# Routed experts after a recurrent layer: two of three groups store their results by tile and gather them by index

## The chip, the cores and the metric

The kernel runs on one core of a Trainium2 chip. The time is device time in microseconds (us) of one execution; "before" is the median of 12 runs. The profile describes one execution taken by the hardware profiler. Engines: TensorE (PE, matmuls; PEld, its weight loads), VectorE (DVE), ScalarE (ACT), GpSimd (POOL), SyncE (SP, here only a queue that issues transfers). Transfers run on 16 DMA engines, whichever queue issues them.

## The reference, cut to what matters

The input is x, 8 sequences of 1024 tokens with 256 features. A first layer (norms, a recurrence along the sequence, a channel mix) is added to x. Then every token is routed to 4 of 32 experts:

```python
x = x + attn_layer(layernorm(x), ...)
xt = layernorm(x).reshape(-1, 256)
gates = sigmoid(xt @ expert_sel.T)                  # 8192 tokens x 32 experts
sel_val, sel_idx = top_k(gates, 4)
gate_full = zeros.at[rows, sel_idx].set(sel_val)
scores = relu(einsum('nd,edf->nef', xt, keys))      # 256 -> 128 per expert
scores = scores * gate_full[:, :, None]
out = einsum('nef,efv->nv', scores, values)         # 128 -> 256, summed over experts
x = x + out
```

Only the chosen four experts of a token need be computed, since the gate of the others is zero. All data is float32.

## The kernel before, in words

The 8192 tokens are 16 blocks of 512. A block passes through the first layer (`norm_a` to `channel_end`), which writes the running x of the block to DRAM (`acc`), and through the routing (`norm_d`, `gates_of`, `rows_of`), which gives each token four rows, one per chosen expert. `post` (line 558) then scatters the normalized token to these rows of a DRAM array `xs`: one indirect transfer on POOL per 128 tokens and choice, 16 per block. In `xs` every expert has a region of its own, so an expert's tokens lie one behind the other. With each token go its place (token number times 4) and its row numbers.

The blocks form three groups of 10, 5 and 1 (`GROUPS`, line 31; the numbers behind the size set the pace). When all blocks of a group are routed, `tile_table` (line 592) works out from the counts which expert and which row of `xs` every tile of 256 rows starts at. A group has 96, 56 and 24 tiles. The last 16 tiles of a group are made of two halves of 128 rows, each with its own expert, so that less is padding; the rows of a tile that are not tokens of its expert are computed as well.

`experts` (line 709) runs the tiles. `fetch` loads a tile from `xs` (SP); `turn` transposes it (TensorE, line 794) and ScalarE (in the first group VectorE) copies it to `xgT` (line 878); `keys` copies the expert's key weights (VectorE, line 785); `hidden` and `result` are the two matmuls (lines 806 and 822), two steps apart, with ScalarE's `hs` (line 884) and `yg` (line 888) between and behind them. `places` (line 762) works out on VectorE, from the row numbers that came with each row, which of the token's four choices it is, and so its row in `ys`, an array with 4 rows per token in token order. `send` (line 832) scatters the 256 results to `ys` with two indirect transfers on POOL, of 128 rows of 1 KB each; rows that are no tokens carry a place out of bounds and are not written.

`combine` (line 892) adds up: for each part of 128 tokens it loads the 4 x 256 results of each token from `ys`, which lie side by side, in one plain transfer of 512 KB (line 909, SP), and adds them with their gates to the block's `acc` (four VectorE instructions, line 917); a finished block goes to the output (line 930; the last block in four pieces, line 927). The sums of a group come after all its tiles, since any tile may hold any token's result.

The order of the work is written as generators: `advance` is called between the pieces of the block loop and moves the background streams (tiles and sums of the groups) by their pace; behind the last block, `drain` runs on until all are done. The tiles of a group follow those of the group before, its sums the sums of the group before. The tile layer then schedules the instructions, each engine runs its own in order, and semaphores join them. `pinned` keeps the tiles of one group in order on each engine; `apart` declares that scatters of one kind need not wait for one another. A read of `ys` waits for all writes of that group's `ys`.

Of the kernel before, what the change touches and what calls it, by code (L numbers as in the profile page):

```python
# [8 lines left out]
F32 = mybir.dt.float32  # L9
BF16 = mybir.dt.bfloat16  # L10
U32 = mybir.dt.uint32
I32 = mybir.dt.int32
AF = mybir.ActivationFunctionType
ALU = mybir.AluOpType
# [5 lines left out]
P = 128  # L20
EPS = 1e-5
WKV_EPS = 1e-8
TOP = 4
# [5 lines left out]


GROUPS = ((10, 6, 2.2, 4, 0.5), (5, 4, 1.6, 4, 0.7), (1, 2, 1.0, 2, 1.0))


@with_exitstack
def rwkv_then_routed_experts(
# [101 lines left out]
    for g, members in enumerate(groups):  # L137
        gt = len(members) * TB
        r = const.tile([P, NE], F32, name=f"region1_{g}")
        nc.gpsimd.iota(  # L140
            r,
            pattern=[[gt + TS, NE]],
            base=TS + 1,
            channel_multiplier=0,
            allow_small_or_imprecise_dtypes=True,
        )
        region1.append(r)
        n_tiles.append(gt * TOP // TS + NE // 2)
        regions.append(NE * (gt + TS))
        xs.append(dram.tile([regions[g] + TS, DX], F32, name=f"xs_{g}"))  # L150
        ys.append(dram.tile([gt * TOP, D], F32, name=f"ys_{g}"))
    tile_no = const.tile([P, 1], F32, name="tile_no")
    nc.gpsimd.iota(
        tile_no, pattern=[[0, 1]], base=0, channel_multiplier=1, allow_small_or_imprecise_dtypes=True
# [340 lines left out]
    def rows_of(i):  # L495
        m = mine[i]
        g = group_of[i]
        chosen = m["chosen"]

        ps = ps_a.tile([P, NT, NE], F32, tag="a", name=f"rank_{i}")  # L500
        prior = counted.get(g)
        nc.tensor.matmul(ps, before, chosen, start=True, stop=False, skip_group_check=True)
        for s in range(1, NT):
            nc.tensor.matmul(
                ps[:, s:, :],
                ones,
                chosen[:, : NT - s, :],
                start=False,
                stop=(s == NT - 1 and prior is None),
                skip_group_check=True,  # L510
            )
        total = p2.tile([P, NT, NE], BF16, tag="total", name=f"total_{i}")
        if prior is not None:
            nc.tensor.matmul(ps, ones, prior, start=False, stop=True, skip_group_check=True)

        key = p2.tile([P, NT, NE], F32, tag="key", name=f"key_{i}")
        nc.vector.tensor_tensor(key, ps, region1[g][:, None, :].to_broadcast([P, NT, NE]), ALU.add)
        nc.vector.tensor_tensor(key, key, chosen, ALU.mult)
        k8 = p2.tile([P, NT, 8], F32, tag="k8", name=f"k8_{i}")
        for t in range(NT):  # L520
            nc.vector.max(k8[:, t, :], key[:, t, :])

        tc.keep_in_program_order(
            nc.vector.tensor_scalar(
                m["x3"][:, :, D], place, float(groups[g].index(i) * TB * TOP), None, ALU.add
            )
        )
        nc.vector.tensor_copy(m["x3"][:, :, D + 1 :], k8[:, :, : TAGS - 1])
        row = p2.tile([P, NT, TOP], U32, tag="row", name=f"row_{i}")
        nc.vector.tensor_scalar(row, k8[:, :, :TOP], -1.0, None, ALU.add)  # L530
        chosen_sum = p2.tile([P, NE], F32, tag="csum", name=f"csum_{i}")
        nc.vector.tensor_reduce(chosen_sum, chosen.rearrange("p t e -> p e t"), AX.X, ALU.add)
        if prior is not None:
            nc.vector.tensor_tensor(chosen_sum, chosen_sum, prior[:, 0, :], ALU.add)
        nc.vector.tensor_copy(total, chosen_sum[:, None, :].to_broadcast([P, NT, NE]))
        counted[g] = total
        m["row"], m["key"], m["k8"] = row, key, k8
# [54 lines left out]
    def tile_table(g):  # L592
# [71 lines left out]
        for k in range(3):  # L664
# [7 lines left out]
        live = small([3], "live")  # L672
        nc.vector.tensor_scalar(live, past[:, :, NE - 1], -1.0, 1.0, ALU.mult, ALU.add)

        say = small([2, 2], "say")
        nc.vector.tensor_copy(say[:, 0, :], what[:, 0, 1:])
        half = small([2], "half")
        nc.vector.tensor_scalar(half, what[:, 1, 1:], float(-regions[g]), None, ALU.add)
# [3 lines left out]
        whole = small([2, 2], "whole")  # L682
        nc.vector.tensor_copy(whole, what[:, :, 0:1].to_broadcast([P, 2, 2]))
        nc.vector.tensor_scalar(whole[:, 1, 1:], whole[:, 1, 1:], float(H), None, ALU.add)
        nc.vector.tensor_tensor(whole, whole, say, ALU.subtract)
        nc.vector.scalar_tensor_tensor(
            say, whole, live[:, 0:1], say, ALU.mult, ALU.add
        )
        yield


        stride = len(groups[g]) * TB + TS
        diag = small([2, P], "diag", BF16)
        ps = ps_a.tile([P, 2, P], F32, tag="a", name=f"all_{g}")
        for k in range(2):
            nc.vector.tensor_scalar(diag[:, k, :], ident, say[:, 0, k : k + 1], None, ALU.mult)
        nc.tensor.matmul(ps, ones, diag, start=True, stop=True)
        limit = p1.tile([P, 2, P], F32, tag="limit", name=f"limit_{g}")
        nc.vector.tensor_scalar(limit, ps, float(stride), float(stride + TS // 2), ALU.mult, ALU.add)

        ps = ps_a.tile([4, P], F32, tag="a", name=f"tr_say_{g}")
        nc.tensor.transpose(ps, say.rearrange("p a b -> p (a b)"), ident)
        table = keep.tile([4, P], I32, name=f"table_{g}")
        nc.vector.tensor_copy(table, ps)
        tables[g] = table, limit

# [2 lines left out]
    def experts(g, pause):  # L709
# [1 line left out]
        table, limit = tables[g]  # L711
        T = n_tiles[g]

        EXPERT, ROW = range(0, 4, 2)
        most = {EXPERT: NE - 1, ROW: regions[g]}
        whole_only = T - NE // 2
        ahead = {}

        def value(t, column, half, engine):

            start = t - t % RUN if t < whole_only else t - (t - whole_only) % RUN
            if (engine, start, column, half) not in ahead:
                stop = min(start + RUN, whole_only if t < whole_only else T)
                _, ahead[engine, start, column, half] = nc.values_load_multi_w_load_instructions(
                    table[column + half : column + half + 1, start:stop],
                    engines=[engine],
                    min_val=0,
                    max_val=most[column],
                    skip_runtime_bounds_check_because=WHY,
                )  # L730
            return ahead[engine, start, column, half][t - start]

        def parts(t):

            return [(0, 0, SJ)] if t < whole_only else [(j, j, j + 1) for j in range(SJ)]

        latest = {}

# [13 lines left out]
        def fetch(t):  # L752
            tag = "xT" if blocks_over and t % 2 else "xg"
            xg = p3.tile([P, SJ, DX], F32, tag=tag, name=f"xg_{g}_{t}")
            for half, j0, j1 in parts(t):
                at = value(t, ROW, half, ET.SP)
                n = j1 - j0
                source = xs[g][bass.ds(at, n * P), :].rearrange("(p j) d -> p j d", j=n)
                nc.sync.dma_start(out=xg[:, j0:j1, :], in_=source)  # L759
            return xg  # L760

        def places(t, xg):
# [53 lines left out]
        def result(t, hs):  # L816
# [12 lines left out]
                    )  # L829
            return ps, last  # L830

        def send(yg, to):
            for j in range(SJ):
                s = nc.gpsimd.indirect_dma_start(  # L834
                    out=ys[g],
                    out_offset=bass.IndirectOffsetOnAxis(ap=to[:, j : j + 1], axis=0),
                    in_=yg[:, j, :],
                    in_offset=None,
                    bounds_check=len(groups[g]) * TB * TOP - 1,
                    oob_is_err=False,  # L840
                )
                apart("store", g, s)
# [15 lines left out]
        for step in range(T + 2 * STAGE):  # L858
# [15 lines left out]
            if step < T:  # L874
                xgT = turned[step] = p3.tile([P, KC, TS], F32, tag="xgT", name=f"xgT_{g}_{step}")

                move = nc.scalar.copy if g else nc.vector.tensor_copy
                after(move(xgT, trx), signal)  # L878
                to[step] = places(step, xg)
            if step < T:  # L880
                ks[step] = keys(step)
            if 0 <= h < T:
# [2 lines left out]
            if 0 <= r < T:  # L885
                tag = "k2" if blocks_over and r % 2 else "yg"
                yg = p3.tile([P, SJ, D], F32, tag=tag, name=f"yg_{g}_{r}")
                after(nc.scalar.copy(yg, po), signal)  # L888
                send(yg, to.pop(r))
            yield  # L890

    def combine(g):
# [10 lines left out]
        def gather(j):  # L903
            i, t = parts[j]
            tags = ("g", "xn", "xa") if blocks_over else ("g",)
            g4 = p2.tile([P, TOP, D], F32, tag=tags[j % len(tags)], name=f"g_{i}_{t}")
            first = TOP * (groups[g].index(i) * TB + t * P)
            rows = ys[g][first : first + TOP * P, :].rearrange("(p k) d -> p k d", k=TOP)
            nc.sync.dma_start(out=g4, in_=rows)  # L909
            got.append((j, [g4[:, k, :] for k in range(TOP)]))  # L910

        def add():
# [167 lines left out]
    for i in range(total_blocks + 1):  # L1080
# [2 lines left out]
                post(len(waiting))  # L1083
                beside(expert_group(g, *pace))
        period(i)
        if i < 2:
            clear(i + 1)
        elif i < 6:
            load_experts(i - 2)
    blocks_over.append(True)  # L1090
    post(len(waiting))
# [47 lines left out]
```

## Time and profile before

| | |
|---|---|
| median of 12 runs | 1382.01 us (1380.36 to 1387.47) |
| the profiled execution | 1384.78 us |
| its span | 1383.1 us |
| busy in the span: PE, DVE, ACT, POOL | 92%, 70%, 42%, 49% |
| indirect transfers on POOL | 352 sends to `ys`, 256 scatters to `xs` |
| plain gathers of sums on SP | 64 |
| PE busy of the 283 us from 1100 | 201.5 us |

Engine rows of the page give tenths of busy time in 40 slices of the span. A group's row gives the line, the engine, the operation and how often; then busy time in us and the mean of one in ns; then the idle time in front and what ended most of it. A row by stretch gives the bounds, the length, the busy time and number of instructions of PE, PEld, DVE, ACT and POOL, the granted TensorE clock (1 is full), the share of the DMA engines' time in use, and GB/s. A row of the timeline gives the start, the duration, the engine and line, and in brackets the idle time before and what ended it. The POOL time of an indirect transfer is the making of its descriptors; its data moves afterwards.

### The profile page before, as it was taken

The numbers are of one execution on the slowest core, as the hardware profiler recorded it, in microseconds if no ns is written. First come the engines' busy times: TensorE is split into PE (matmuls) and PEld (weight loads), VectorE is DVE, ScalarE is ACT, GpSimd is POOL, SyncE is SP. The second block draws the span as 40 slices with busy tenths as digits, with TensorE's granted clock in tenths as the row PEclk, the third lists the DMA queues.
The fourth block names the chain that finished last, engine by engine and source line by source line (L and its number), as shares of the span: only waits on it lengthen the run. The fifth ranks groups of instructions, "written<-read, shape, count | busy, mean of one in ns | idle before, by whom it ended". The sixth has DMA issues, their size and how long they took to land. (4 is left out here: it accounts for less than half of the span.)

```text
span 1383.1 us, 19513 instructions
## 1 busy us (share of the span) xinstructions
PE 1267.1 (92%) x5590; PEld 916.2 (66%) x5590; DVE 971.4 (70%) x3166; ACT 586.6 (42%) x1122; POOL 671.5 (49%) x678
## 2 busy tenths in 40 slices
PE   6999999999999999998999999999998578688772
PEld 2566666666666666665877787787875367577662
DVE  6957878878878878878666667766656847356484
ACT  3354444444444544543444434434434144345431
POOL 2011433333423422535476667667656437777763
PEclk9999999999999999999999999999998879899896
DMA  9990221421411211213465455445337669798595
GB/s 326 343 287 4 86 109 46 146 103 48 150 47 43 90 47 43 90 44 121 121 196 160 146 155 189 153 144 176 109 129 254 229 216 322 275 309 275 202 310 208
DMA packets 134074, 223.06 MB, mean 161 GB/s; under 512 B 19231, under 2 KB 92229, under 8 KB 133456
## 3 DMA queue, kind: packets, MB, share of 16 engines
q1 hardware_dynamic: 102736, 151.96, 35.1%
q0 software_dynamic: 29184, 68.25, 13.4%
q10 hardware_dynamic: 2048, 1.61, 0.4%
q8 instruction: 46, 0.75, 0.2%
q14 instruction: 60, 0.49, 0.1%
HBM read 110.01 MB, written 124.28 MB: 169 GB/s over the span
## 5 line engine op out<-in xcount | busy, mean ns | idle before, releaser
L834 POOL DMA_INDIRECT ys<-yg,to x352 | 352.4, 1001 | 197.8 <-ACT yg L888 85.7
L563 POOL DMA_INDIRECT xs<-x,row x256 | 257.4, 1005 | 102.2 <-issue 85.4
L423 PEld LDWEIGHTS cm<-wval,k 128*128 128x128 f32 x1024 | 194.3, 190 | 77.0 <-issue 50.0
L244 PE MATMUL pj_f<-xT,wkey 128*128 128x512 f32 x512 | 243.9, 599 | 0.0
L423 PE MATMUL cm<-wval,k 128*128 128x256 f32 x1024 | 240.5, 379 | 2.3 <-ACT k L416 2.3
L806 PE MATMUL ph<-xgT,key 128*128 128x256 f32 (+1 forms) x896 | 190.9, 345 | 18.0 <-DVE key L785 10.2
L822 PE MATMUL po<-wexp,hs 128*128 x704 | 186.0, 387 | 5.7 <-ACT hs L884 4.9
L917 DVE SCALAR_TENSOR_TENSOR ac<-g,gate,ac 128x256 f32<-128x256 f32 x256 | 123.1, 487 | 84.7 <-DMA g<-ys 67.0
L806 PEld LDWEIGHTS ph<-xgT,key 128*128 128x128 f32 x896 | 151.5, 197 | 39.5 <-issue 16.4
L371 POOL TENSOR_TENSOR x<-x,xa 128x1024 f32<-128x1024 f32 x16 | 37.9, 2368 | 255.6 <-issue 222.8
L415 ACT ACTIVATE k<-pj_f 128x512 f32<-128x512 f32 x128 | 76.5, 598 | 195.7 <-PE pj_f L244 195.7
L822 PEld LDWEIGHTS po<-wexp,hs 128*128 128x128 f32 x704 | 125.2, 194 | 27.2 <-issue 8.1
L244 PEld LDWEIGHTS pj_f<-xT,wkey 128*128 128x128 f32 x512 | 92.9, 191 | 68.4 <-issue 65.5
L794 PE MATMUL trx<-ident,xg 128*128 128x128 f32 x704 | 110.3, 282 | 28.8 <-ACT xgT L878 18.5
L884 ACT ACTIVATE hs<-ph 128x256 f32<-128x256 f32 x176 | 68.4, 389 | 154.0 <-PE trx L794 148.6
L888 ACT COPY yg<-po 128x512 f32<-128x512 f32 x176 | 102.7, 584 | 68.9 <-DMA ys<-yg,to 67.8
L878 DVE COPY xgT<-trx 128x512 f32<-128x512 f32 x96 | 65.6, 683 | 84.5 <-PE trx L794 84.5
L794 PEld LDWEIGHTS trx<-ident,xg 128*128 128x128 f32 x704 | 89.5, 146 | 47.2 <-ACT xgT L878 21.8
L325 DVE RECIPROCAL rw<-rw 128x512 f32<-128x512 f32 x32 | 107.3, 3353 | 1.0
L785 DVE COPY key<-wexp 128x256 f32 x224 | 69.2, 319 | 45.7 <-PE ph L806 32.0
L878 ACT COPY xgT<-trx 128x512 f32<-128x512 f32 x80 | 47.0, 589 | 83.6 <-PE trx L794 83.6
L416 ACT ACTIVATE k<-k 128x512 f32<-128x512 f32 x128 | 80.6, 630 | 4.1
(162 smaller groups left out, 1735.0 us busy)
## 6 DMA issues: line engine op xcount, KB each, us to landing
xg<-xs SPq DMA_DIRECT2D x128, 264.0 KB
g<-ys SPq DMA_DIRECT2D x64, 512.0 KB
xs<-zeros SPq DMA_DIRECT2D x6, 4224.0 KB
xg<-xs SPq DMA_DIRECT2D x96, 132.0 KB
x<-in_x SPq DMA_DIRECT2D x16, 512.0 KB
acc<-x SPq DMA_DIRECT2D x16, 512.0 KB
wexp<-in_w_exp SPq DMA_DIRECT2D x4, 2048.0 KB
ac<-acc SPq DMA_DIRECT2D x16, 512.0 KB
```

What stands on the lines that cost most here:

```text
L244: nc.tensor.matmul(ps, w(c), rhs[:, c, :], start=(c == 0), stop=(c == KC - 1))
L325: inverse = nc.vector.reciprocal(rc, rc)
L416: nc.scalar.activation(k2, k2, AF.Square)
L423: nc.tensor.matmul(m["cm"][t // 2][:, t % 2, :], k2[:, t * P : (t + 1) * P], wval[:, f, :], start=(f == 0 and t % 2 == 0), stop=(f == FC - 1),
L563: s = nc.gpsimd.indirect_dma_start(out=xs[g], out_offset=bass.IndirectOffsetOnAxis(ap=m["row"][:, t, k : k + 1], axis=0), in_=m["x3"][:, t ...
L794: nc.tensor.transpose(ps[:, c, j * P : (j + 1) * P], xg[:, j, c * P : (c + 1) * P], ident)
L806: nc.tensor.matmul(ps[:, cols], key[:, c * P : (c + 1) * P], xgT[:, c, cols], start=(c == 0), stop=(c == KC - 1),)
L822: nc.tensor.matmul(ps[:, j, :], hs[:, j * P : (j + 1) * P], wexp[:, bass.ds(e, 1), KC * P :], start=True, stop=True,)
L834: s = nc.gpsimd.indirect_dma_start(out=ys[g], out_offset=bass.IndirectOffsetOnAxis(ap=to[:, j : j + 1], axis=0), in_=yg[:, j, :], in_offse ...
L878: after(move(xgT, trx), signal)
L888: after(nc.scalar.copy(yg, po), signal)
L917: nc.vector.scalar_tensor_tensor(ac, gk, routed[i][:, t, k : k + 1], ac, ALU.mult, ALU.add)
```

## The change

For groups two and three (`PLAIN = (1, 2)`):

- `ys` has the layout of `xs`: a tile's 256 results are stored in the rows that its inputs came from, with plain transfers on ScalarE's queue, one of 256 KB for a whole tile and two of 128 KB for a tile of two halves. Padding rows are stored too. Tiles that hold nothing get rows of their own behind the regions (`dead`, `PLACE`); a third pair of columns in the table gives the row.
- `places` and the `limit` table are not made, and `send` is not called.
- The row numbers of each block (`row`) are kept, and `combine` gathers a part of 128 tokens with four indirect transfers on POOL, one per choice, of 128 rows of 1 KB each, where it had one plain load on SP.

Group one is as before.

```diff
+PLAIN = (1, 2)
...
-        ys.append(dram.tile([gt * TOP, D], F32, name=f"ys_{g}"))
+        results = regions[g] + n_tiles[g] * TS if g in PLAIN else gt * TOP
+        ys.append(dram.tile([results, D], I32 if g in PLAIN else F32, name=f"ys_{g}"))
...
-        row = p2.tile([P, NT, TOP], U32, tag="row", name=f"row_{i}")
+        if g in PLAIN:
+            row = keep.tile([P, NT, TOP], U32, name=f"row_{i}")
+        else:
+            row = p2.tile([P, NT, TOP], U32, tag="row", name=f"row_{i}")
...
+        if g in PLAIN:
+
+            dead = small([2], "dead")
+            nc.vector.tensor_scalar(
+                dead, past[:, 1:, NE - 1], past[:, 0, NE - 1 : NE], None, ALU.mult
+            )
+            nc.vector.tensor_tensor(dead, dead, down, ALU.mult)
+            nc.vector.tensor_tensor(say[:, 2, :], say[:, 1, :], dead, ALU.add)
         yield
...
+        def store(t, yg):
+            for half, j0, j1 in parts(t):
+                at = value(t, PLACE, half, ET.Activation)
+                s = nc.scalar.dma_start(out=rows(ys[g], at, j1 - j0), in_=yg[:, j0:j1, :].bitcast(I32))
+                apart("store", g, s)
...
-                to[step] = places(step, xg)
+                if g not in PLAIN:
+                    to[step] = places(step, xg)
...
-                send(yg, to.pop(r))
+                if g in PLAIN:
+                    store(r, yg)
+                else:
+                    send(yg, to.pop(r))
...
-            first = TOP * (groups[g].index(i) * TB + t * P)
-            rows = ys[g][first : first + TOP * P, :].rearrange("(p k) d -> p k d", k=TOP)
-            nc.sync.dma_start(out=g4, in_=rows)
+            if g in PLAIN:
+                for k in range(TOP):
+                    nc.gpsimd.indirect_dma_start(
+                        out=g4[:, k, :].bitcast(I32),
+                        out_offset=None,
+                        in_=ys[g],
+                        in_offset=bass.IndirectOffsetOnAxis(ap=mine[i]["row"][:, t, k : k + 1], axis=0),
+                    )
+            else:
+                first = TOP * (groups[g].index(i) * TB + t * P)
+                rows = ys[g][first : first + TOP * P, :].rearrange("(p k) d -> p k d", k=TOP)
+                nc.sync.dma_start(out=g4, in_=rows)
```

More of the change, by code (lines that the diff above doesn't have):

```diff
@@ L673, in tile_table @@
         nc.vector.tensor_scalar(live, past[:, :, NE - 1], -1.0, 1.0, ALU.mult, ALU.add)
-        say = small([2, 2], "say")
+        say = small([3, 2], "say")
         nc.vector.tensor_copy(say[:, 0, :], what[:, 0, 1:])
@@ L684, in tile_table @@
         nc.vector.tensor_scalar(whole[:, 1, 1:], whole[:, 1, 1:], float(H), None, ALU.add)
-        nc.vector.tensor_tensor(whole, whole, say, ALU.subtract)
+        nc.vector.tensor_tensor(whole, whole, say[:, :2, :], ALU.subtract)
         nc.vector.scalar_tensor_tensor(
-            say, whole, live[:, 0:1], say, ALU.mult, ALU.add
+            say[:, :2, :], whole, live[:, 0:1], say[:, :2, :], ALU.mult, ALU.add
         )
-        yield
-        stride = len(groups[g]) * TB + TS
-        diag = small([2, P], "diag", BF16)
@@ L694, in tile_table @@
[L694 to L702, printed above, removed]
@@ L703, in tile_table @@
-        table = keep.tile([4, P], I32, name=f"table_{g}")
+        if g in PLAIN:
[5 more added lines that the diff above has]
+            nc.vector.tensor_tensor(say[:, 2, :], say[:, 1, :], dead, ALU.add)
+        yield
+        limit = None
+        if g not in PLAIN:
+            stride = len(groups[g]) * TB + TS
+            diag = small([2, P], "diag", BF16)
+            ps = ps_a.tile([P, 2, P], F32, tag="a", name=f"all_{g}")
+            for k in range(2):
+                nc.vector.tensor_scalar(diag[:, k, :], ident, say[:, 0, k : k + 1], None, ALU.mult)
+            nc.tensor.matmul(ps, ones, diag, start=True, stop=True)
+            limit = p1.tile([P, 2, P], F32, tag="limit", name=f"limit_{g}")
+            nc.vector.tensor_scalar(
+                limit, ps, float(stride), float(stride + TS // 2), ALU.mult, ALU.add
+            )
@@ L704, in tile_table @@
+        columns = 6 if g in PLAIN else 4
+        ps = ps_a.tile([columns, P], F32, tag="a", name=f"tr_say_{g}")
+        nc.tensor.transpose(ps, say.rearrange("p a b -> p (a b)")[:, :columns], ident)
+        table = keep.tile([columns, P], I32, name=f"table_{g}")
         nc.vector.tensor_copy(table, ps)
@@ L712, in experts @@
         T = n_tiles[g]
-        EXPERT, ROW = range(0, 4, 2)
-        most = {EXPERT: NE - 1, ROW: regions[g]}
+        EXPERT, ROW, PLACE = range(0, 6, 2)
+        most = {EXPERT: NE - 1, ROW: regions[g], PLACE: regions[g] + (T - 1) * TS}
         whole_only = T - NE // 2
@@ L727, in value @@
                     min_val=0,
-                    max_val=most[column],
+                    max_val=most[column] + (half * TS // 2 if column == PLACE else 0),
                     skip_runtime_bounds_check_because=WHY,
@@ L735, in parts, with rows @@
             return [(0, 0, SJ)] if t < whole_only else [(j, j, j + 1) for j in range(SJ)]
+        def rows(array, at, n):
+            return array[bass.ds(at, n * P), :].rearrange("(p j) d -> p j d", j=n)
         latest = {}
@@ L757, in fetch @@
                 n = j1 - j0
-                source = xs[g][bass.ds(at, n * P), :].rearrange("(p j) d -> p j d", j=n)
-                nc.sync.dma_start(out=xg[:, j0:j1, :], in_=source)
+                nc.sync.dma_start(out=xg[:, j0:j1, :], in_=rows(xs[g], at, n))
             return xg
@@ L878, in experts @@
                 after(move(xgT, trx), signal)
-                to[step] = places(step, xg)
+                if g not in PLAIN:
+                    to[step] = places(step, xg)
             if step < T:
@@ L906, in gather @@
             g4 = p2.tile([P, TOP, D], F32, tag=tags[j % len(tags)], name=f"g_{i}_{t}")
-            first = TOP * (groups[g].index(i) * TB + t * P)
-            rows = ys[g][first : first + TOP * P, :].rearrange("(p k) d -> p k d", k=TOP)
-            nc.sync.dma_start(out=g4, in_=rows)
+            if g in PLAIN:
[5 more added lines that the diff above has]
+                        in_offset=bass.IndirectOffsetOnAxis(ap=mine[i]["row"][:, t, k : k + 1], axis=0),
+                    )
+            else:
+                first = TOP * (groups[g].index(i) * TB + t * P)
+                rows = ys[g][first : first + TOP * P, :].rearrange("(p k) d -> p k d", k=TOP)
+                nc.sync.dma_start(out=g4, in_=rows)
             got.append((j, [g4[:, k, :] for k in range(TOP)]))
@@ L1085, in rwkv_then_routed_experts @@
         period(i)
-        if i < 2:
+        if i + 1 < len(groups):
             clear(i + 1)
-        elif i < 6:
+        elif 2 <= i < 6:
             load_experts(i - 2)
```

## The prediction

> **What bounds the kernel now.** I read the page first (engine shares, forty slices), then the chain that ended last, then busy time by stretch of the last 270 us, then the waits and the timelines there. Up to 1050 us TensorE is busy nearly all the time and nothing that the change touches lies there. The last quarter is different:
>
> ```profile
> span 1383.1 us, 19513 instructions
> ...
> PE   6999999999999999998999999999998578688772
> ...
> POOL 2011433333423422535476667667656437777763
> PEclk9999999999999999999999999999998879899896
> DMA  9990221421411211213465455445337669798595
> ...
> DMA ys<-yg,to 4%; DMA g<-ys 3%; PE ph L806 2%; DVE ac L917 1%; PE po L822 1%; POOL ys L834 1%; PE trx L794 1%; DMA out<-ac 1%; SPq L759 0%; DMA ac<-acc 0%; DVE key L785 0%; DMA xg<-xs 0%; ACT xgT L878 0%; SPq L909 0%; POOL xs L563 0%
> ...
> L834 POOL DMA_INDIRECT ys<-yg,to x352 | 352.4, 1001 | 197.8 <-ACT yg L888 85.7
> ```
>
> The reader is to see TensorE fall from 9 to 5 to 8 tenths in the last nine slices, and the indirect sends `ys<-yg,to` at the head of the chain. By stretch (start and end; PE, PEld, DVE, ACT, POOL busy; clock, DMA share, GB/s):
>
> ```profile
> 1125.80:1189.40 63.60, 55.29 (x300) 47.16 (x297) 42.49 (x213) 29.90 (x66) 48.46 (x48) 0.97 0.93 315
> 1189.40:1295.10 105.70, 84.70 (x491) 73.31 (x492) 48.27 (x194) 50.24 (x110) 80.98 (x82) 0.94 0.75 250
> 1295.10:1366.50 71.40, 48.69 (x278) 41.80 (x276) 49.58 (x165) 25.40 (x57) 47.72 (x47) 0.88 0.86 296
> 1366.50:1383.10 16.60, 0.00 (x0) 0.00 (x0) 7.23 (x16) 0.00 (x0) 0.00 (x0) 0.50 0.45 163
> ```
>
> POOL runs 130 indirect DMAs from 1125.8 to 1295.1: 129.4 us busy plus 130 gaps of 0.30 us is the whole stretch. Its timeline shows the pitch, 1.28 us, and the waits of this stretch show who pays:
>
> ```profile
> 1190.69 0.98 POOL L834 DMA_INDIRECT ys<-yg,to  x1 [0.30 <-issue]
> 1191.98 0.97 POOL L834 DMA_INDIRECT ys<-yg,to  x1 [0.30 <-issue]
> ```
> ```profile
> ACT yg L888 <- DMA ys<-yg,to: 67.8, 37, 11.2
> ```
>
> So the second group's 56 tiles are bound by POOL's sends: ScalarE waits 67.8 us for result buffers. The hand-over follows: last result copy of that group, first gather of its sums, last additions of all.
>
> ```profile
> 1280.50 0.59 ACT L888 COPY yg<-po 128x512 f32<-128x512 f32 x1 [2.91 <-DMA ys<-yg,to]
> ```
> ```profile
> 1295.10 0.33 SPq L909 DMA_DIRECT2D g<-ys  x1
> ```
> ```profile
> 1376.20 4.03 DVE L917 SCALAR_TENSOR_TENSOR ac<-g,gate,ac 128x256 f32<-128x256 f32 x9 [1.50 <-DMA g<-ys]
> ```
>
> Call T1 the time at which all results of the second group have landed: 1295 now. From T1 to the end now takes 88 us, because its sums are fetched by 20 plain loads of 512 KB that SP issues at 0.43 us each.
>
> **The change, part by part.**
>
> *Removed from POOL:* 112 sends of group two and 48 of group three. *Added to POOL:* 80 gathers for group two (5 blocks x 4 parts x 4) and 16 for group three. The count falls by 64, but in time it is a move: the removed ones ran beside the tiles, while no gather can start before T1, since it reads rows that any tile may have stored. In the built order of the changed kernel all 96 gathers stand at the end of POOL's queue, behind the last scatters.
>
> *T1.* Without the sends three things can hold the 56 tiles. TensorE: the result copies on ScalarE stand 2.17 us apart where nothing waits (1124.93, 1127.09), so 1124.9 + 55 x 2.17 = 1244; with the last block's gate products (1.7 us), the copy (0.6), two issues (0.9) and a landing (2.4 to 5.4 us as the sends show), T1 = 1250 to 1253. DMA: 1120 to 1280 moves 46.9 MB at 293 GB/s. The plain stores write all 256 rows of a tile, 56 x 0.262 = 14.7 MB, where the sends wrote the 10,240 real rows, 10.5 MB: 4.2 MB more. Some 3.9 MB (fetches of group three, sums of group two) may slide behind, leaving 47.2 MB: at the 345 GB/s of the fullest 10 us stretches 137 us, at the present mean 161, so the last copy comes at 1257 to 1281 and T1 at 1261 to 1286. ScalarE: a tile takes 1.35 us now; one store adds 0.43 (its issues in the first 6 us), a half tile two, so 1.8 to 2.3 us with a wait for its own copy, about TensorE's pace; 14 table loads at 0.54 to 0.6 are 8 us, mostly in slack. I take T1 = 1272, in the middle of the DMA bound, 23 us earlier than now; ends 1250 and 1286.
>
> The Trainium skill, page "DMA: Bandwidth & Descriptors", section "Issuing engines are not separate DMA queues", says that issuing from another engine saves only the issue time, usually small beside the transfer. By that rule moving the stores to ScalarE's queue would leave T1 near 1295; here the issue is what POOL is full of, and no run shows yet which of the two holds.
>
> *Gathers of group two.* The trace has no gather by index. The nearest row is the scatter by index: also 128 rows of 1 KB per instruction, pitch 1.28 us. A plain issue (0.33 to 0.43 us) is the lower bound, the longest scatter (1.91 + 0.30) the upper: over the 94 pitches below, minus 80 or plus 87 us. I take 1.28, as the scatters of both kinds agree (medians 0.962 and 0.974). First gather at 1272.1, the 80th at + 79 x 1.28 = 1373.2. Six buffers hold the gathered parts; an addition of a part takes 4 x 0.49 against 5.1 us for its gathers, so POOL is never held by them. Now the same rows come in 60 us beside the sends; that cover is gone.
>
> Page "SBUF — State Buffer", section "SBUF: two separate sides", says that a VectorE copy in a two-port mode keeps POOL from writing descriptors. Its figures, about 620 ns alone and 3100 overlapped, would add an estimated 40 x 2.5 = 100 us if each of the 40 key copies met a gather; the sends beside the same copies show a mean of 1.00 and a longest of 1.91 us.
>
> *What is queued behind a waiting addition.* On VectorE the additions of group two stand between the key copies of group three: key 5 behind two additions, keys 20 to 23 behind all 80. TensorE's later stages wait for those keys, so the third group's tiles now run at the gathers' pace, and the last four only start when the 80th gather has landed (2.4 us) and been added (0.5). Then: two key copies 0.6; TensorE 4 hidden x 0.86, 2 transposes x 0.66, 6 results x 0.86 = 9.9 at full clock (groups of four in the chain); ScalarE 1.0; two issues 0.9; landing 2.4; plus 1.7 because the clock stands at 0.50 to 0.54 after idle (1110 to 1120, 1190 to 1200). That is 16.5; with TensorE at half clock throughout 25, and 1.3 for the whole gap if POOL could go straight on. So gather 81 comes 19.4 us after gather 80: 1392.6. Third group: 15 x 1.28 = 19.2, to 1411.8.
>
> *End.* Landing 2.4, last addition 0.5, output 2.9 (now from the last addition at 1380.2 to 1383.1): 1417.6.
>
> *At nothing:* 240 small VectorE instructions that worked out places (0.16 us each) and the two limit tables are gone, a few for the third pair of table columns are new; VectorE is busy half of these stretches. The kept row tiles cost memory only. SP loses 24 loads of 0.43, behind no one.
>
> Sum: span 1417.6 against 1383.1, plus 34.5. The profiled run took 1384.78, 1.68 outside the span and 2.77 above the median 1382.01. On the median: 1416.5.
>
> **Rivals.**
>
> *Cheap gathers (not slower).* If POOL writes a gather's descriptors faster than a scatter's, the whole tail shrinks by 94 us per us of pitch. It decides at 1.28 - 34.5/94 = 0.91 us with my T1, at 1.15 with T1 = 1250. At 0.8: 1371. For it: the fall of 64 instructions and POOL being the bound. Against: both scatters cost the same whatever their target, so the work seems to be the 128 descriptors.
>
> *The sends were hidden anyway.* The DMA share is already 0.93 in the first stretch; if the larger stores fill what the sends left, T1 stays at 1290: 1416.5 + 18 = 1434. Against: 0.75 in the second stretch.
>
> *Dear gathers.* Reads of scattered rows beside busy VectorE and DMA at a pitch of 1.6: 94 x 0.32 = + 30, 1446.
>
> *Third group not held.* If its tiles finish before gather 80, the gap is 1.3: 1398. Against: the order on VectorE.
>
> **How the numbers follow.** Main case 0.68, its own range 1394 to 1431 (T1 alone gives minus 22 to plus 14). Sends hidden 0.11, dear gathers 0.09, third group not held 0.05, cheap gathers 0.07. About 0.2% (2.8 us) is what a measurement of this kernel tells from no change. Cheap gathers fall mostly below it: faster 0.06, same 0.02, slower 0.92. Range 1393 to 1446: it leaves out cheap gathers and half of the dear ones.
>
> **What would show it.** Right: POOL empty or nearly so from the last scatter to about 1272, then 80 gathers in a row near 1.28 us, a hole of some 20 us, 16 more; ScalarE's wait for `ys` gone; TensorE thin after T1 with its clock below 0.8; VectorE waiting for gathers. Wrong: a pitch below 1.15 us, a T1 above 1290 or below 1250, or no hole before the last 16.

## The result, and the profile after

The changed kernel takes 1423.11 us (median of 8 runs, 1422.06 to 1427.63) against 1383.35 us of the kernel before, measured beside it: a ratio of 1.0291, 95% interval 1.0279 to 1.0303. It is 2.9% slower. The profiled execution took 1428.24 us, its span 1426.2 us. In the changed code `turn` is at line 815, `keys` at 806, `hidden` at 827, the store at 856, `send` at 861, `xgT`, `hs` and `yg` at 905, 912 and 916, the gather by index at 940 and the addition at 957.

The page of the changed kernel, rows as in the one of before:

```profile
span 1426.2 us, 19276 instructions
...
PE   6999999999999999999999999999986788884661
...
POOL 2011343244144144172666666676663040007754
PEclk9999999999999999999999999999998799997676
DMA  9980230331321121124555455444377799977853
...
q10 hardware_dynamic: 18176, 22.59, 4.4%
...
L940 POOL DMA_INDIRECT g<-ys,row x96 | 93.2, 970 | 155.8 <-DMA ys<-yg 107.6
```

POOL, which ran at 7 tenths where the second group's tiles were sent, is now at 0 there and at 7 behind it: the work has moved from beside the tiles to behind them. The 96 gathers take 970 ns each. The last stretches, with the columns of the prediction's table (length; PE, PEld, DVE, ACT, POOL busy; clock, DMA share, GB/s):

```profile
1125.80:1189.40 63.60, 56.30 (x311) 47.33 (x309) 30.77 (x125) 31.67 (x70) 16.52 (x16) 1.00 0.98 347
1189.40:1279.60 90.20, 74.71 (x421) 63.83 (x422) 34.32 (x98) 42.68 (x94) 0.00 (x0) 0.95 0.92 306
1279.60:1401.30 121.70, 72.22 (x333) 60.31 (x331) 46.72 (x115) 30.67 (x68) 78.03 (x81) 0.75 0.67 208
1401.30:1426.20 24.90, 0.00 (x0) 0.00 (x0) 7.75 (x16) 0.00 (x0) 15.12 (x16) 0.50 0.37 106
```

In the first two, POOL runs nothing but the last 16 scatters, and the DMA engines are in use for 0.92 to 0.98 of the time; behind 1279.6 they have slack and POOL is what is full. POOL's timeline shows the three parts of the tail; these are the first two gathers, the 80th and 81st, and the last:

```profile
1279.62 0.99 POOL L940 DMA_INDIRECT g<-ys,row  x1 [107.58 <-DMA ys<-yg]
1280.91 0.96 POOL L940 DMA_INDIRECT g<-ys,row  x1 [0.30 <-issue]
...
1380.76 0.94 POOL L940 DMA_INDIRECT g<-ys,row  x1 [0.30 <-issue]
1401.29 0.94 POOL L940 DMA_INDIRECT g<-ys,row  x1 [19.58 <-issue]
...
1420.04 0.95 POOL L940 DMA_INDIRECT g<-ys,row  x1 [0.30 <-issue]
```

So: 79 pitches in 101.14 us, a hole of 20.53 us between two starts, 15 pitches in 18.75, and 6.2 us from the last start to the end of the span. The span grew by 43.1 us. T1, the start of the sums, came 15.5 us earlier (1295.1 to 1279.6); from T1 to the end it is 146.6 us instead of 88.0, which is 58.6 more.

VectorE's timeline shows what the hole is made of:

```profile
1383.83 0.48 DVE L957 SCALAR_TENSOR_TENSOR ac<-g,gate,ac 128x256 f32<-128x256 f32 x1 [0.44 <-DMA g<-ys,row]
1384.23 0.89 DVE L806 COPY key<-wexp 128x256 f32 x4
```

The key copies of tile 20 come right behind the last addition of group two; the last result copy follows at 1397.59 and its two stores at 1398.20. The second of them has landed at 1400.45, and the gathers of the third group start at 1401.29.

The waits from 1110 us to the end (us in total, times, longest):

```profile
POOL g L940 <- DMA ys<-yg: 107.6, 1, 107.6
DVE ac L957 <- DMA g<-ys,row: 79.6, 72, 13.5
...
POOL g L940 <- issue: 44.9, 84, 19.6
PE ph L827 <- DVE key L806: 42.8, 17, 6.5
...
ACT xgT L905 <- DMA xg<-xs: 20.9, 5, 9.6
...
ACT yg L916 <- DMA ys<-yg: 4.8, 2, 2.6
```

ScalarE's wait for result buffers fell from 67.8 to 4.8 us. VectorE's additions wait for the gathers, TensorE's `hidden` for the key copies behind those additions.

### The profile page after: what moved, and what is told of

Its sections match the earlier page's. It is cut to its first block, busy times and chain, and to the rows that moved or that the text cites. A ratio compares the mean times of both kernels' runs of the same rounds, so it can differ in the third digit from the quotient of the medians.

```text
span 1426.2 us, 19276 instructions
## 1 busy us (share of the span) xinstructions
PE 1281.6 (90%) x5588; PEld 925.8 (65%) x5588; DVE 945.0 (66%) x2926; ACT 586.1 (41%) x1122; POOL 603.7 (42%) x614
## 5 line engine op out<-in xcount | busy, mean ns | idle before, releaser
L861 POOL DMA_INDIRECT ys<-yg,to x192 | 190.9, 994 | 121.7 <-ACT yg L916 54.5
L827 PE MATMUL ph<-xgT,key 128*128 128x256 f32 (+1 forms) x896 | 196.9, 353 | 45.8 <-DVE key L806 43.2
L843 PE MATMUL po<-wexp,hs 128*128 x704 | 191.6, 396 | 17.0 <-ACT hs L912 13.1
L827 PEld LDWEIGHTS ph<-xgT,key 128*128 128x128 f32 x896 | 156.0, 203 | 70.7 <-issue 37.5
L940 POOL DMA_INDIRECT g<-ys,row x96 | 93.2, 970 | 155.8 <-DMA ys<-yg 107.6
L843 PEld LDWEIGHTS po<-wexp,hs 128*128 128x128 f32 x704 | 128.1, 198 | 40.5 <-ACT hs L912 17.0
## 6 DMA issues: line engine op xcount, KB each, us to landing
xs<-zeros SPq DMA_DIRECT2D x6, 4224.0 KB, 19.7
```

Source lines behind the costliest of these rows:

```text
L827: nc.tensor.matmul(ps[:, cols], key[:, c * P : (c + 1) * P], xgT[:, c, cols], start=(c == 0), stop=(c == KC - 1),)
L843: nc.tensor.matmul(ps[:, j, :], hs[:, j * P : (j + 1) * P], wexp[:, bass.ds(e, 1), KC * P :], start=True, stop=True,)
L861: s = nc.gpsimd.indirect_dma_start(out=ys[g], out_offset=bass.IndirectOffsetOnAxis(ap=to[:, j : j + 1], axis=0), in_=yg[:, j, :], in_offse ...
L940: nc.gpsimd.indirect_dma_start(out=g4[:, k, :].bitcast(I32), out_offset=None, in_=ys[g], in_offset=bass.IndirectOffsetOnAxis(ap=mine[i]["r ...
```

## The experiments

Times are compared on the chip where they were taken. Four runs (`keys_first`, `half_gathers`, `third_only`, `second_only`) fell on a chip that is slower with every kernel: the one before takes 1502.88 us there, and the block stages, which no edit touches, are longer too. Of these only ratios to the kernel before and lengths of stretches are used. The other chips give 1382.17 and 1383.65 us for the kernel before.

**The unaltered changed kernel, as a control.**

> The changed kernel once more, unaltered, beside three that differ from it in one thing each, on one chip. Its ratio to the kernel before was 1.029. Every theory expects 1.025 to 1.035, and the same three parts after the last store of group two has landed: 80 gathers 1.28 us apart (101 us), a hole of about 20 us, 16 gathers (19 us).

Measured: 1425.77 us, ratio 1.0306 (1.0286 to 1.0326). Its first gather is at 1280.32, the hole between two starts ends at 1401.84, and the last gather starts at 1420.65: the same parts as above, within 1 us. T1 itself varies more: the next experiment, whose edit acts only behind T1, has it at 1276.18.

**The key copies of group three ahead of the additions of group two.** Only the order on VectorE is altered; nothing is left out.

```diff
+                key_made[g, t] = pinned(nc.vector.tensor_copy(key, ...))
...
+                if g == 1:      # addition of part j
+                    tc.add_manual_dep(added.ins, key_made[2, min(23, 6 + 2 * j)].ins.name, NoSync, ...)
```

> The changed kernel, with the additions of group two ordered on VectorE so that all key copies of group three come before the additions of the tenth part. Theory (the 96 gathers run in series on POOL, and the last four tiles of group three wait for the 80th gather through VectorE's order): T1 stays near 1280, the 80 gathers still take 101 us, the hole before the last 16 shrinks from 20.5 us to 1 to 4, and the span falls by 16 to 19 us, from 1426 to 1407 to 1410. Rival (group three's tiles are late for another reason: DMA, the granted clock, or their fetches): the hole stays above 12 us and the time moves by less than 8 us.

> The changed kernel, with the additions of group two's part j behind the key copy of tile 6 + 2j of group three, beside the unaltered one. Theory (the hole comes from the keys behind the additions): the hole of 20 us is gone, some of it paid back in waits of the gathers for their buffers, 0 to 15 us; so 5 to 20 us less than the unaltered kernel, a ratio of 0.986 to 0.997 between the two. Rival (TensorE and the transfers of group three need that time wherever its keys stand): within 0.3% of the unaltered kernel.

Measured beside the control: 1406.09 us against 1425.77, 0.986 of it; to the kernel before 1.0177 (1.0150 to 1.0204). That is 19.7 us less, at the favourable end of what was expected. In the timeline of POOL (the gather is at line 941 here) the first and the last of 96 gathers are

```profile
1276.18 1.02 POOL L941 DMA_INDIRECT g<-ys,row  x1 [105.07 <-DMA xg<-xs]
...
1396.69 0.95 POOL L941 DMA_INDIRECT g<-ys,row  x1 [0.30 <-issue]
```

that is 120.5 us for 95 pitches, 1.27 us each: there is no hole, and no gather waits for a buffer. Between the 80th and the 81st start there is one pitch instead of the control's 19.91 us, 18.6 us less, which is nearly all of the gain. By stretch:

```profile
1276.10:1300.00 23.90, 23.90 (x149) 21.81 (x148) 10.23 (x29) 13.46 (x30) 18.31 (x19) 0.98 0.93 296
1300.00:1330.00 30.00, 26.45 (x176) 24.11 (x176) 15.86 (x44) 14.79 (x35) 22.84 (x23) 0.94 0.96 309
1330.00:1360.00 30.00, 2.33 (x11) 1.42 (x10) 10.48 (x24) 2.42 (x6) 22.84 (x24) 0.58 0.64 197
```

TensorE's last instruction of group three ends at 1333; in the changed kernel the last four of these tiles only start behind the addition at 1383.83. So the third group's tiles fit beside the gathers of the second; the hole came from the queue on VectorE, and the rival, that the time is needed anyway, falls.

On the slower chip the same edit gave 1.0074 (1.0048 to 1.0100) of the kernel before there. The hole is gone too, but POOL pays some of it back; there its waits say

```profile
POOL g L941 <- DVE key L807: 23.8, 5, 7.2
```

where the gathers stood for buffers that additions behind late key copies held. With the chip at its usual pace this wait does not appear.

**What sets the start of the gathers: the stores on another queue, and fewer bytes.**

```diff
-                at = value(t, PLACE, half, ET.Activation)
-                s = nc.scalar.dma_start(...)
+                at = value(t, PLACE, half, ET.Pool if g == 1 else ET.Activation)
+                s = (nc.gpsimd if g == 1 else nc.scalar).dma_start(...)
```

> The changed kernel, with the plain stores of group two issued on POOL's queue, which is nearly empty there, instead of ScalarE's. Theory (the start of the gathers is set by the bytes that the transfers move, 0.92 to 1.04 of their time): first gather and time within 4 us of the unaltered kernel (0.3%). Rival (it is set by ScalarE, which stands at a store until its result copy and an earlier transfer are done, while the other copies of the tiles queue behind): first gather about 15 us earlier, and so the time (ratio 0.99 to the unaltered kernel).

```diff
-                nc.sync.dma_start(out=g4, in_=rows)
-            got.append((j, [g4[:, k, :] for k in range(TOP)]))
+                nc.sync.dma_start(out=g4[:, :2, :], in_=rows[:, :2, :])
+            got.append((j, [g4[:, k, :] for k in range(TOP if g else 2)]))
```

> The changed kernel, which leaves out two of the four choices in the sums of group one: its plain loads fetch half as much, some 5.5 MB less between the last scatter and the first gather. Theory (bytes set the start of the gathers): 5.5 MB at 345 GB/s is 16 us, so the first gather 10 to 16 us earlier against the unaltered kernel, and the time too (ratio 0.989 to 0.993). Rival (ScalarE or TensorE sets it): first gather and time within 4 us.

Measured: the stores on POOL's queue 1418.14 us, 0.9946 of the control, 1.0256 (1.0239 to 1.0273) of the kernel before; with fewer bytes 1413.93 us, 0.9917 of the control. The first gathers, of the control, of the stores on POOL's queue and of fewer bytes, stand at

```profile
1280.32 0.98 POOL L940 DMA_INDIRECT g<-ys,row  x1 [106.82 <-DMA xg<-xs]
```
```profile
1267.30 1.02 POOL L940 DMA_INDIRECT g<-ys,row  x1 [4.90 <-DMA xg<-xs]
```
```profile
1265.74 0.98 POOL L940 DMA_INDIRECT g<-ys,row  x1 [99.32 <-DMA xg<-xs]
```

that is 13.0 and 14.6 us earlier than in the control. Each is from one execution; the medians fell by 7.6 and 11.8 us. I had set these two against one another, and had expected the first to move nothing. Both move T1, so neither alone was the bound. (With fewer bytes half of group one's additions are left out too, and VectorE works 46.7 us instead of 65.2 from 1125.8 to 1265. That can hardly be the cause: in the control TensorE waits for key copies for only 1.2 us before T1.) The stretch from 1125.8 to 1265, first of the control and then of the stores on POOL's queue, shows how:

```profile
1125.80:1265.00 139.20, 120.24 (x677) 102.07 (x675) 65.17 (x220) 67.90 (x151) 16.35 (x16) 0.98 0.98 341
```
```profile
1125.80:1265.00 139.20, 127.40 (x746) 110.86 (x745) 66.01 (x224) 74.88 (x166) 55.33 (x87) 0.98 0.99 356
```

The DMA share is 0.98 in one and 0.99 in the other, yet the second moved 356 GB/s instead of 341, and TensorE did 7.2 us more work in the same time. What holds the first is ScalarE at its stores. Its timeline in the changed kernel:

```profile
1239.30 0.59 ACT L916 COPY yg<-po 128x512 f32<-128x512 f32 x1
1239.92 3.79 ACTq L856 DMA_DIRECT2D ys<-yg  x2
1243.76 0.59 ACT L905 COPY xgT<-trx 128x512 f32<-128x512 f32 x1 [3.86 <-DMA xg<-xs]
```

One issue takes 0.34 to 0.41 us, but these two stores, of two halves of one result that was complete at 1239.89, last 3.79 us, and the next tile's copy comes only behind them. The trace records for which counts an instruction waits. In the changed kernel 66 of the 72 stores of group two wait, beside their own copy, for the completion count of an earlier transfer: the queues of SP and ScalarE share eight such counts. Twenty of the 72 are issued within 0.15 us of the landing of that transfer, in 17 cases one of SP's queue, and ScalarE stands idle for 31.7 us ahead of these twenty (29.6 in the control, also ahead of twenty). The second store of the rows above is one of them: a fetch of `xg` landed 0.02 us before its issue.

Added up from the timeline of the changed kernel (from the end of the ScalarE instruction ahead of a store to the end of its issue, 1125.8 to 1278 us), the 72 stores take 59.3 us of ScalarE, of which 72 x 0.38 = 27 is issue and 32 waiting; in the control 56.3 and 29. With the stores on POOL's queue these waits are off the engine that has the tiles' copies to make; POOL's transfers have counts of their own, and no store there is issued within 0.15 us of such a landing. With fewer bytes the waits are shorter (24 by the same sum).

On POOL's queue the same bytes go in fewer packets (4736 instead of 10368 for the 72 stores), but not at a lower price: from 1125.8 to 1265 the stores took 24.6% of the DMA engines' time for 12.81 MB in the control and 28.1% for 14.63 MB on POOL's queue (without its scatters), 1.92% per MB in both. What the stores' place on ScalarE costs is 9 to 13 us of T1: with the same bytes, three executions with it have T1 at 1276.2 to 1280.3, two without it at 1267.2 and 1267.3. That the waits are for the shared counts the trace shows; no run takes away the counts alone.

**Both edits.** The two diffs above in one kernel, the stores of group two on POOL's queue and the keys of group three first:

> The changed kernel with both edits: the stores of group two on POOL's queue, and the additions of group two behind the key copies of group three. If the two losses are separate, they add: first gather at about 1267 us, then 96 gathers without a hole, 95 x 1.27 = 121 us, and 6 us to the end: a span of about 1394 us, a ratio of 1.010 to the kernel before (1.005 to 1.014). Rival (the earlier gathers meet the transfers of group three, and wait for them): no better than the keys alone, 1.018.

Measured: 1398.70 us, ratio 1.0107 (1.0093 to 1.0122); gathers from 1267.16 to 1387.97 without a hole. The separate gains, 19.7 and 7.6 us, add to 27.3; from the control's 1425.77 that is 1398.5, so the two losses are separate. What is left of the loss is the 96 gathers in a row at 1.27 us behind T1.

**Half the gathers of group two, and one group alone.** These are of the slower chip.

```diff
-                for k in range(TOP):
+                for k in range(TOP if g == 2 else 2):
...
-            got.append((j, [g4[:, k, :] for k in range(TOP)]))
+            got.append((j, [g4[:, k, :] for k in range(2 if g == 1 else TOP)]))
```

> The changed kernel without the gathers and additions of the third and fourth choice of group two: 40 of 96 gathers are left out, and the output lacks those terms. Theory: what follows T1 is POOL's series, so the span falls by 40 x 1.27 = 51 us to about 1375, T1 unchanged near 1280, the 40 gathers end at about 1331, and the hole before the last 16 stays near 20 us or grows by a few, since group three's tiles now come at TensorE's pace. Rival (something else sets the time after T1): the span falls by less than 25 us.

Measured, in one run: 1487.94 us, 0.990 of the kernel before there. Group two's gathers end sooner, but then the hole is twice as long; by stretch, gathers of group two, hole, end:

```profile
1356.00:1417.40 61.40, 27.15 (x127) 22.38 (x126) 18.63 (x46) 11.67 (x26) 38.62 (x40) 0.69 0.62 191
1417.40:1459.10 41.70, 32.52 (x209) 29.08 (x207) 8.85 (x29) 19.00 (x42) 0.05 (x1) 0.95 0.62 202
1459.10:1486.00 26.90, 0.00 (x0) 0.00 (x0) 7.75 (x16) 0.00 (x0) 15.12 (x16) 0.50 0.35 98
```

The ratio is near what the theory gives (a span of 1375 against 1383.1), but not by its parts: from the first gather to the end 130.2 us passed, where the theory has 95. In the hole TensorE is busy for 32.5 of 41.7 us: more of the third group's tiles are left when the additions are done. Part of that is this chip: ScalarE stood for 24.6 us in a wait that the trace marks as remote, until 1404.6, and TensorE for 21.7 us behind it. So the size of the hole is not to be taken over, and since the changed kernel was not run here, the run does not say what a gather left out is worth.

```diff
-PLAIN = (1, 2)
+PLAIN = (2,)
```

> Only group three is stored by tile; group two keeps its sends and plain loads. Theory (group two's late gathers are the loss; the change to group three costs about what it saves): T1 is back at 1290 to 1296, group two's sums are loaded beside group three's tiles, group three's last store lands near 1360 because DMA is full there, then 16 gathers of 1.25 us and 6 us for the end: span 1380 to 1390, within 0.5% of the kernel before. Rival (storing by tile is itself what costs, whatever the group): 1395 or more.

> Only group two is stored by tile; group three keeps its 48 sends and 4 plain loads. Theory (POOL's queue after T1 sets the end): T1 near 1280, then 80 gathers and 48 sends share POOL, 128 x 1.27 = 163 us to about 1443, then 12 to 16 us for the last loads and additions: span 1450 to 1465, the slowest of all. Rival (the late gathers of group three and the hole before them are the loss): the hole goes and the span falls to 1400 to 1415.

Measured: the third group alone 1.0049 (1.0027 to 1.0072) of the kernel before, just within the theory's 0.5%; the second alone, in one run, 1550.40 us or 1.032. That lies between the theory (a span of 1450 or more, 1.048) and the rival (1415 or less, 1.023). With the second alone (`PLAIN = (1,)`) the 48 sends of group three stay on POOL among the 80 gathers, as the timeline there shows:

```profile
1400.67 0.97 POOL L940 DMA_INDIRECT g<-ys,row  x1 [0.30 <-issue]
1401.94 1.01 POOL L861 DMA_INDIRECT ys<-yg,to  x1 [0.30 <-ACT hs L912]
1403.26 0.99 POOL L861 DMA_INDIRECT ys<-yg,to  x1 [0.30 <-issue]
1404.55 1.09 POOL L940 DMA_INDIRECT g<-ys,row  x1 [0.30 <-issue]
```

A gather and a send cost about the same here, 0.97 and 1.09 us against 0.99 and 1.01. The third group alone loses little, and the second alone loses here what both lose elsewhere (1.029 and 1.031). That points to the second group; it is not shown, since the changed kernel was not run on this chip and the second alone has 48 sends among its gathers.

**The keys first in the kernel before.** If the order on VectorE costs the changed kernel 20 us, it may cost the kernel before something, where POOL waits 12.0 us for results of group three between 1290 and 1366 us. Only the order is altered, as above, with two paces.

```diff
+                        key_made[2, min(23, 6 + 2 * j)].ins.name,        # before_keys_first
+                        key_made[2, min(23, 6 + 3 * j // 2)].ins.name,   # before_keys_gentle
```

> The kernel before, with nothing of the change, and only the additions of group two's part j behind the key copy of tile 6 + 2j of group three. Theory (the key copies behind additions cost the kernel before too: POOL waits 12 us there for results of group three's tiles between 1290 and 1366 us): its last sends come 5 to 10 us earlier, 1373 to 1378 us, ratio 0.993 to 0.997. Rival (that stretch is bound by the transfers, 0.86 of their time, so that the sums only come later): 0.998 to 1.005.

> As the run with the keys first in the kernel before, but part j behind the key copy of tile 6 + 1.5j, so that the sums start sooner and the keys are less far ahead. Theory: POOL waits less than 12 us but more than with 2j, the sums are done earlier: ratio 0.992 to 0.997, within 0.3% of the other. Rival (bound by the transfers): 0.998 to 1.002.

Measured: 1381.47 us, 0.9975 (0.9963 to 0.9987), and 1377.44 us, 0.9952 (0.9940 to 0.9964). The first lies between what theory and rival expected, the second where the theory had it. The gentler one is faster than both kernels, by 6.2 us against the one before. POOL's waits for result copies between 1290 and 1366 us, of the kernel before and then of the gentler version:

```profile
POOL ys L834 <- ACT yg L888: 12.0, 8, 4.2
```
```profile
POOL ys L835 <- ACT yg L889: 0.6, 2, 0.3
```

The last send starts at 1355.52 instead of 1365.46, and the span is 1375.6 instead of 1383.1. The transfers were at 0.91 of their time from 1295.1 to 1360 and are at 0.93: they did have some room. In the faster pace one send took 6.43 us where all others take about 1:

```profile
1342.80 6.43 POOL L835 DMA_INDIRECT ys<-yg,to  x1 [0.30 <-issue]
```

and its last send starts at 1363.08. What such a long one comes from was not tried; that it explains the difference between the two paces is not shown, since only one execution of each has a trace.

**The third group alone, with its keys first.** The diff of the keys in a kernel with

```diff
-PLAIN = (1, 2)
+PLAIN = (2,)
```

> Only group three stored by tile and gathered by index (PLAIN = (2,), which was 1.005 without more), and the additions of group two behind its key copies. Theory (the 16 gathers then come while the sums of group two still run, so their 20 us and the hole are covered): ratio 0.994 to 1.001. Rival (the third group's larger stores keep the transfers full to the end, 0.9 to 1.0 of their time in the run without the keys): 1.002 to 1.008.

Measured: 1395.04 us, 1.0073 (1.0049 to 1.0097), where the rival had it. The 16 gathers did not come beside the sums. The trace puts the wait of the first, until 1367.79, to an addition that frees a buffer; but the last store of the third group landed only at 1366.93, so a free buffer would have gained less than 1 us. The transfers were full meanwhile:

```profile
POOL g L941 <- DVE ac L958: 76.2, 3, 75.6
```
```profile
1320.00:1345.00 25.00, 21.23 (x133) 18.48 (x132) 11.73 (x32) 10.80 (x24) 0.00 (x0) 0.93 1.01 335
1345.00:1365.00 20.00, 9.32 (x57) 7.63 (x56) 16.17 (x41) 6.85 (x15) 0.00 (x0) 0.85 0.99 324
```

## Why the prediction was right, point by point

The main case came true: 1423.1 against 1416.5, inside its own range. The profiled span is 1426.2 against the sum's 1417.6, 8.6 us more, which go to these terms:

| step | predicted | measured |
|---|---|---|
| T1, first gather | 1272.1 (1250 to 1286) | 1279.6 |
| 79 pitches | 101.1 | 101.1 |
| hole, gather 80 to 81 | 19.4 | 20.5 |
| 15 pitches | 19.2 | 18.75 |
| last gather to the end | 5.8 | 6.2 |

- *T1* is the term that was mis-sized, by 7.5 us. The step that failed is that of ScalarE: "one store adds 0.43 (its issues in the first 6 us), a half tile two, so 1.8 to 2.3 us with a wait for its own copy, about TensorE's pace". A store also waits for another transfer, and the 72 stores took 59 us of ScalarE where 72 x 0.43 would be 31. The DMA step, which I took instead, had the rate right: from 1125.8 to T1 the changed kernel moved 49.7 MB at 323 GB/s, within the bounds of 293 and 345. Its bytes were short: from 1120 to the last result copy, which ended at 1275, 50.1 MB were moved where the step had 47.2, so about 1 MB slid behind instead of 3.9. The 2.9 MB more are 9 us at that rate, about the size of the miss. And I had treated the limits as alternatives of which the largest counts; the two runs and the waits for shared counts show that each held the other up. That T1 came out within 7.5 us is in part luck, since the middle of the DMA bound stood in for a coupling that the sum does not have.
- *The pitch.* The nearest row, the scatter, was the right one: 1.28 us predicted, 1.280 measured over 79 pitches. Cheap gathers (below 0.91 us) and dear ones (1.6) did not occur. The fall from 352 sends to 192 and 96 gathers was worth nothing as a count.
- *The hole* was predicted from the order on VectorE, with its size from the stages behind it, and the runs with the keys first take it away. The third group was held.
- *Sends hidden anyway* (T1 at 1290) did not occur, though T1 lies nearer to it than I took it: the DMA share of the two stretches rose from 0.93 and 0.75 to 0.98 and 0.92.
- *At nothing*: the 240 small VectorE instructions and SP's loads. Nothing in the runs asks for a price for them; they were not tried alone.
- The Trainium skill, page "DMA: Bandwidth & Descriptors", section "Issuing engines are not separate DMA queues", says that another queue saves only the time of issuing, usually small; by the prediction's reading T1 would have stayed near 1295. Here T1 moved by 15.5 us with the sends off POOL, which was full of them. It moved by another 9 to 13 when the plain stores left ScalarE, and there it was waits that were saved and not issue, which the page does not count.
- Page "SBUF — State Buffer", section "SBUF: two separate sides": the 2.5 us that the prediction worked out from its figures for each meeting of a gather with a key copy are not seen. The longest of the 96 gathers took 1.20 us, the mean was 0.97. The key copies last only 0.29 us each, so these rows do not show what a longer copy would do.

## What to carry to other kernels

Moving a transfer by index from the producing side to the consuming side moves its descriptor time too; ask on which side it ran beside other work, and count it at its full pitch where it cannot start before the last producer. Where a consumer's instruction that waits for slow transfers stands in an in-order queue ahead of cheap work of the next stage, put the cheap work first: that was worth 1.4% in the changed kernel and 0.25% or 0.5%, by its pace, in the one before, and it needed no other change. A transfer that is issued from an engine with work of its own can cost that engine the waits of the transfer and not only the issue: here 32 of 59 us.

## What was not expected

A DMA share near 1 did not mean that no more could be moved: 0.98 and 0.99 stood for 341 and 356 GB/s in the same stretch, with the same stores on another queue. And single indirect transfers of 6.43 and 6.04 us occurred on POOL (one in the kernel before with the keys first, one in the changed kernel with the keys first on the slower chip), among others of 0.94 to 1.3 in the same stretch; no run here tells why.
